# A graph network with routed experts: one row a node sent twice, shares computed beside the slots, a matrix loaded ahead of the last fronts

## The chip, the core and the metric

The kernel runs on one core of a Trainium2 chip. The metric is the device time of one execution in microseconds, the median over runs; less is better.

## What is computed

The reference adds eight layers to `x` (3125 nodes, 256 features), each on a normalized `x`. Graph layers and feed-forward layers alternate:

```
x = x + _L0_gnn_ref(_layernorm(x), edge_index, ...)   # attention, 4 heads, with loops
x = x + _L0_ffn_ref(_layernorm(x)[None], ...)[0]      # 8 experts, hidden 256, best 2, shares by softmax
x = x + _L1_gnn_ref(...)                              # two attention layers
x = x + _L1_ffn_ref(...)                              # a recurrence over all nodes
x = x + _L2_gnn_ref(...)                              # three convolutions
x = x + _L2_ffn_ref(...)                              # 8 experts, hidden 1024, own norm each, best 2, shares
x = x + _L3_gnn_ref(...)                              # one convolution
x = x + _L3_ffn_ref(...)                              # 8 experts, hidden 512, best 2, no shares
```

An expert layer picks for each node the two experts with the highest scores and adds their outputs, weighted by the shares where there are shares. Three blocks have experts: the first, the third and the fourth.

## The kernel before

Nodes lie in 25 tiles of 128 rows, the last with 53. `x` stays on the chip. A program fixes the order of the work: instructions run in order on each engine, and the pieces of different steps are laid between each other by hand, as lists of small functions.

**Fronts** (`Experts.front`, L2075). As soon as a graph layer has finished some node tiles, the front of the expert layer takes them: `norm` normalizes the rows into a tile `rows` (L2071), `turn` transposes them for the scores and makes a second copy of the row on ScalarE (L2098), `route` finds the best two experts (L2104 to L2125), `place` counts the nodes in front of each one and gives every choice a row of the table `slots` in device memory (L2127 to L2149), and `send` writes the two copies of a row there, by two indirect transfers of POOL for a tile (L2194). Each copy carries in its last column the row of `results` that its output goes to (L2149). The table has 3328 rows for each expert. `clear` (L2184) zeroes the rows behind each expert's last one. The sends use eight views of the table in turn, and a transfer waits until the one before it in the same view has landed. A front takes four tiles in the first block (`few=4`, one buffer of `rows`) and two in the others (two buffers). A buffer can be written again when its sends have landed.

**Where the fronts run.** In the first block they are pieces in the list `rest` that `sweep` pops between steps of the attention, and in POOL's queue their sends stand among the gathers of edges (L1826). `finish_apart` starts one when four tiles are done, `finish` when a group of four is (L931 to L972). The first tiles of the attention are dense matmuls (L903, L909) on values that VectorE makes (L846); the other tiles are gathered. In the third and fourth blocks `convolve_rows` (L1388) gives each piece a step of its loop at which it is due. What is left at the end of the loop comes after it (L1444). Then `plan` (L2301) computes the schedule of slots (`schedule`, L2206) and the shares (`weights`, L2276).

**Slots** (`Experts.run`, L2306). There are 56 slots of 128 rows. A loop has five steps, each for another slot: `load` reads the rows by SP at a place that `schedule` gave (L2339), `turn` transposes them, `expand`, `grow` and `shrink` are the two matmuls with the Gelu between (L2380, L2397, L2405), and POOL scatters the output to `results` (L2411). Afterwards the results are read back and added with the shares (L2455).

**Weights.** `open_weights(0)` loads the first matrices of all experts during the graph layer, eight transfers by SP (L2050). The fourth block loads the second ones then too. In the first and third block the second matrices don't fit beside the graph layer's tiles, and `run` loads them, ahead of the first slot in SP's queue.

Of the kernel before, what the change touches and what calls it, by code (L numbers as in the profile page):

```python
# [32 lines left out]
P = 128  # L33
# [22 lines left out]
EACH = NP + P  # L56
FOUR = 4
# [24 lines left out]
class Net:  # L82
    def __init__(self, ctx, tc, w, out):
# [19 lines left out]
        self.slots = dram.tile([E * EACH, D + 1], F32, name="slots")  # L103
# [775 lines left out]
    def attend4(self, ctx, name, psum, hv, target, loops, need, flag, done, rows, times,  # L879
# [52 lines left out]
        def finish_apart(t, acc):  # L932
# [3 lines left out]
            first = t - (t - apart.start) % 4  # L936
            if ready and (t == NT - 1 or t - first == 3):
                apart.rest += ready(psum, first, t - first + 1)
# [4 lines left out]
        def finish(t0, n, acc):  # L943
# [26 lines left out]
            if ready:  # L970
                pieces += ready(psum, t0, n)
# [44 lines left out]
    def gnn0(self, experts):  # L1016
        nc, x = self.nc, self.x
        with ExitStack() as ctx:
# [5 lines left out]
            with ExitStack() as inner:  # L1024
# [11 lines left out]
                z = pc.tile([P, D + 1], F32, name="z")  # L1036
# [39 lines left out]
            with ExitStack() as inner:  # L1076
# [5 lines left out]
                experts.plan(self.pool(inner, "g0plan", 1))  # L1082
# [305 lines left out]
    def convolve_rows(self, cpool, accp, loops, hs, done, ready, loads, apart=None):  # L1388
# [55 lines left out]
        for _, piece in loads + waiting:  # L1444
            piece()

    def gcn(self, name, weights, biases, loops, experts, gather=True):
# [3 lines left out]
        with ExitStack() as ctx:  # L1451
            c = self.pool(ctx, name + "const", 1)
            last = self.pool(ctx, name + "hs", 1)
            cpool = self.pool(ctx, name + "c", 3)
            accp = self.pool(ctx, name + "acc", 2, space=PSUM)
            psum = self.pool(ctx, name + "ps", 3, space=PSUM)
            places = Gathered.pools(self, ctx, name) if gather else None
            shape, kind = ([P, NT, PARTS, D], BF16) if gather else ([P, NT, D], F32)
            experts.begin(ctx)
            inner = ctx.enter_context(ExitStack())  # L1460
# [133 lines left out]
            self.convolve_rows(cpool, accp, loops, hs, add, ready, loads, apart)  # L1594
# [355 lines left out]
class Experts:  # L1950
# [11 lines left out]

    def __init__(self, net, ctx, name, hid, router, w1, b1, w2, b2, bias=None, gain=None,
                 shift=None, keep_tokens=False, weighted=True, store=False,
                 few=2):
# [4 lines left out]
        self.ctx, self.few, self.mats = ctx, few, [None, None]  # L1970
# [22 lines left out]
        self.rows_to = c.tile([P, NT, 2], F32, name="rowsto")  # L1993
        nc.gpsimd.iota(
            self.rows_to, pattern=[[2 * P, NT], [1, 2]], base=0, channel_multiplier=2,
# [5 lines left out]
        self.regs = c.tile([1, SLOTS, 4], I32, name="regs")  # L2001


        if few != 2:
            self.zeros = c.tile([P, FOUR * (D + 1)], F32, name="zeros")
            nc.vector.memset(self.zeros, 0.0)
# [28 lines left out]
    def begin(self, ctx):  # L2035

        self.wk = self.net.pool(ctx, self.name + "front", 2)
        self.big = self.net.pool(ctx, self.name + "frontrows", 4 // self.few)
# [21 lines left out]
    def normalized(self, src, dsts):  # L2060

        nc, n = self.nc, len(src)
        mv = self.wk.tile([P, self.few, 2], F32, name="mv")
# [11 lines left out]
    def front(self, psum, t0, n):  # L2075
# [126 lines left out]
        if self.sent == NT:  # L2202
            pieces.append(clear)
# [97 lines left out]
    def plan(self, pool):  # L2301

        self.schedule(pool)
        self.weights(pool)
# [290 lines left out]
```

## Time and profile before

| | us |
|---|---|
| median of 4 runs | 5177.46 |
| lowest, highest | 5167.13, 5186.29 |
| the profiled execution | 5172.7 |
| its span, first to last instruction | 5170.9 |
| first block: sweep's last matmul, first slot loaded | about 905.5, 969.2 |
| third block: last matmul of the convolution, first matmul of a slot | about 3796.8, 3855.8 |
| fourth block: first slot loaded | 4821.0 |
| slot loops of blocks 1, 3, 4 | about 970 to 1165, 3858 to 4385, 4825 to 5116 |

In a timeline a line is: start, length, engine, source line, operation, output<-input, count, and in brackets how long the engine was idle before and what ended it. In the chain a line is: start, length, what the time went to. "issue" is waiting that the profile can't put down to anything. SPq is SP's queue. Instruction names carry the kernel's tile names: `rows<-x` writes a front's rows, `slots<-rows` sends them, `slots<-slots` loads a slot.

### The profile page before, as it was taken

The page shows a single profiled execution, that of the slowest core. Times are in us where ns is not written, and L with a number is a line of the kernel's source. Part 1 is how long each engine was busy: PE and PEld are TensorE (multiplying, and loading weights), DVE is VectorE, ACT ScalarE, POOL GpSimd, SP SyncE. Part 2 cuts the span into 40 slices and gives each one's busy share as a digit, 9 for nine tenths or more (in the row PEclk, how much of TensorE's full clock was granted, in tenths as well). Part 3 has the DMA queues.
Part 4 walks back from the last instruction along what each step waited for, and adds up shares of the span by engine and source line. Part 5 has one row for each costly group of instructions (what it writes and reads, how often), then busy time and mean ns, then how long its engine had stood idle before and what let it go on. Part 6 is the DMA issues. An engine that isn't in the chain of part 4 may idle for free. (4 is left out here: it accounts for less than half of the span.)

```text
span 5170.9 us, 79417 instructions
## 1 busy us (share of the span) xinstructions
PE 4138.0 (80%) x29365; PEld 2351.5 (45%) x29365; DVE 2431.2 (47%) x7697; ACT 1030.7 (20%) x3048; POOL 1715.7 (33%) x1662
## 2 busy tenths in 40 slices
PE   5867788586998799999998778787649998666795
PEld 3434343453444466744444434344325555433453
DVE  8945555446555455676677311114342222523333
ACT  2411111221011100243333101000013333100231
POOL 2067774223766263000001343534521111344211
PEclk8888888797999899999998988888769999778897
DMA  3243333233333444000000344444431112534213
GB/s 110 81 133 96 97 90 70 89 89 111 109 94 89 97 129 96 2 2 2 2 2 26 110 122 120 127 135 148 108 115 33 30 29 82 156 109 101 57 50 102
DMA packets 351817, 433.30 MB, mean 84 GB/s; under 512 B 74454, under 2 KB 286114, under 8 KB 351427
## 3 DMA queue, kind: packets, MB, share of 16 engines
q0 software_dynamic: 78720, 213.50, 15.2%
q1 hardware_dynamic: 249491, 191.44, 12.7%
q10 hardware_dynamic: 23216, 23.17, 1.4%
q8 instruction: 244, 4.00, 0.3%
q14 instruction: 146, 1.20, 0.1%
HBM read 341.19 MB, written 88.37 MB: 83 GB/s over the span
## 5 line engine op out<-in xcount | busy, mean ns | idle before, releaser
L1826 POOL DMA_INDIRECT edge<-scored,from x780 | 856.5, 1098 | 682.2 <-issue 207.5
L1906 POOL DMA_INDIRECT edge<-rows,from x480 | 460.5, 959 | 477.5 <-PE edgeacc L1941 209.9
L1862 PE MATMUL edgeacc<-edge,weight 128*32 128x65 f32 (+1 forms) x5280 | 424.4, 238 | 145.6 <-issue 110.3
L1862 PEld LDWEIGHTS edgeacc<-edge,weight 128*32 128x32 f32 x5280 | 347.1, 115 | 265.6 <-issue 175.6
L2411 POOL DMA_INDIRECT results<-y,to x168 | 163.7, 974 | 873.5 <-DVE y L2410 680.7
L2405 PE MATMUL py<-w,ht 128*128 x1568 | 429.1, 388 | 13.5 <-DVE y L2410 8.4
L1370 PE MATMUL acc<-c,hs 128*128 128x512 bf16 (+1 forms) x1500 | 374.2, 391 | 60.7 <-issue 59.1
L1648 PE MATMUL pz<-lstm_v,hist 128*32 128x192 f32 x7120 | 384.2, 334 | 26.7 <-DVE hist L1746 7.2
L2380 PE MATMUL ph<-w,xt 128*128 x896 | 387.9, 566 | 20.9 <-ACT xt L2362 14.9
L1415 PE MATMUL acc<-hs,c 128*128 128x512 bf16 x950 | 359.8, 418 | 55.2 <-issue 55.0
L2397 ACT ACTIVATE ht<-pt,par 128x128 f32<-128x128 f32 x784 | 267.5, 367 | 435.2 <-PE pt L2394 425.7
L1419 PE MATMUL acc<-hs,c 128*128 128x256 bf16 x950 | 278.8, 294 | 43.3 <-issue 42.5
L2405 PEld LDWEIGHTS py<-w,ht 128*128 128x128 f32 x1568 | 258.1, 190 | 67.8 <-DVE y L2410 26.9
L2194 POOL DMA_INDIRECT slots<-rows,sloti x150 | 157.5, 1050 | 366.4 <-DVE sloti L2148 188.8
L1681 PE MATMUL pz<-pre,ident 128*128 128x192 f32 x900 | 269.3, 382 | 11.4 <-PEq L1754 11.4
L1648 PEld LDWEIGHTS pz<-lstm_v,hist 128*32 128x32 f32 x7120 | 186.4, 109 | 179.8 <-DVE hist L1746 147.0
L1370 PEld LDWEIGHTS <-hs 128*128 128x128 bf16 x1500 | 150.2, 102 | 254.8 <-issue 124.5
L1773 POOL MEMSET hall<- 128x128 f32 x1 | 0.2, 205 | 788.2 <-DMA L_gnn_b<-in_L_gnn_b 788.2
L2385 DVE COPY h<-ph 128x512 f32<-128x512 f32 (+1 forms) x224 | 139.9, 625 | 216.0 <-PE ph L2380 193.5
L2380 PEld LDWEIGHTS ph<-w,xt 128*128 128x128 f32 x896 | 159.1, 193 | 174.0 <-issue 116.0
L991 PE MATMUL acc<-g1bhv,v 128*128 128x257 f32 x850 | 203.8, 395 | 20.7 <-DVE v L846 13.2
L846 DVE SCALAR_TENSOR_TENSOR v<-q,g1ahv,c 128x512 f32<-128x512 f32 (+1 forms) x300 | 197.0, 702 | 45.2 <-PE acc L909 28.6
(477 smaller groups left out, 6311.2 us busy)
## 6 DMA issues: line engine op xcount, KB each, us to landing
c<-ct SPq DMA_DIRECT2D x106, 640.0 KB
slots<-slots SPq DMA_DIRECT2D x168, 128.5 KB
got<-results SPq DMA_DIRECT2D x24, 768.0 KB
w<-in_L_ffn_W SPq DMA_DIRECT2D x16, 1024.0 KB
ct<-cols SPq DMA_DIRECT2D x6, 2400.0 KB
c<-ct SPq DMA_DIRECT2D x30, 480.0 KB
edge<-scored,from POOLq DMA_INDIRECT x780
rows<-new ACTq DMA_DIRECT2D x20, 512.0 KB
```

What stands on the lines that cost most here:

```text
L991: nc.tensor.matmul(a[:, : D + 1], v[0][:, j * P : (j + 1) * P], hv[:, s, 0, : D + 1], start=(s == 0), stop=(s == NT - 1),)
L1370: made = self.nc.tensor.matmul(acc[f][:, : n * P], lhs, cols[s], start=(s == 0 and i == 0), stop=(s == NT - 1), skip_group_check=True,)
L1415: nc.tensor.matmul(acc[t], lhs, hs[:, s, 0:2, :].rearrange("p i d -> p (i d)"), start=start, stop=stop, skip_group_check=True,)
L1419: return nc.tensor.matmul(acc[t][:, D:], lhs, hs[:, s, 2, :], start=False, stop=stop, skip_group_check=True,)
L1648: made = nc.tensor.matmul(pz[q * R : (q + 1) * R, :], s, m, start=start, stop=stop, tile_position=(0, q * R),)
L1681: made = nc.tensor.matmul(pz, self.ident, pre[:, g, s, :], start=True, stop=False)
L1826: nc.gpsimd.indirect_dma_start(out=tile[:, j, :], out_offset=None, in_=self.rows, in_offset=bass.IndirectOffsetOnAxis(ap=index, axis=0),)
L1862: nc.tensor.matmul(state["acc"][g * GROUP : (g + 1) * GROUP, at : at + width + 1], m[:, j, h, :], rows[:, j, h, : width + 1], start=(j == ...
L1906: self.net.nc.gpsimd.indirect_dma_start(out=tile, out_offset=None, in_=self.rows, in_offset=bass.IndirectOffsetOnAxis(ap=index, axis=0),)
L2380: nc.tensor.matmul(ph[:, :wide], st["xt"][:, k, :], st["w1"][:, k * hid + c0 : k * hid + c0 + wide], start=(k == 0), stop=(k == KD - 1),)
L2397: nc.scalar.activation(ht[:, m, :], pt[:, cut], AF.Gelu, bias=st["par"][:, m : m + 1])
L2405: nc.tensor.matmul(py[:, :D], st["ht"][:, m, :], st["w2"][:, m * D : (m + 1) * D], start=(m == 0), stop=(m == nhc - 1),)
```

## The change

A row is kept once, with two more columns instead of one: the result row of the first choice, and the table row of the second. Both sends of a node send the same row. In the slot loop a new VectorE instruction compares the second column with the slot's own table rows (`self.numbers`, computed in `schedule`) and adds 1 to the result row where they are equal. `rows` has three buffers everywhere, in a pool of its own. All fronts take two tiles (`PAIR`). `clear` comes after the last sends, with a tile of zeros of its own. `weights` moves into the slot loop, at its sixth turn (`i == 5`). In the first block the second matrix is loaded after the second slot. In the third block the convolution's tiles are released as soon as its last matmuls are in the program, and the second matrix is loaded there, ahead of the pieces of fronts that are left.

```diff
-            first = t - (t - apart.start) % 4
-            if ready and (t == NT - 1 or t - first == 3):
+            first = t - (t - apart.start) % PAIR
+            if ready and (t == NT - 1 or t - first == PAIR - 1):
                 apart.rest += ready(psum, first, t - first + 1)
...
-            if ready:
-                pieces += ready(psum, t0, n)
+            for j in range(0, n if ready else 0, PAIR):
+                pieces += ready(psum, t0 + j, min(PAIR, n - j))
...
-                experts.plan(self.pool(inner, "g0plan", 1))
+                experts.schedule(self.pool(inner, "g0plan", 1))
...
-        for _, piece in loads + waiting:
-            piece()
+        return [piece for _, piece in loads + waiting]
...
-            self.convolve_rows(cpool, accp, loops, hs, add, ready, loads, apart)
+            rest = self.convolve_rows(cpool, accp, loops, hs, add, ready, loads, apart)
+            held.close()
+            if loops:
+                rest = experts.open_weights(1) + rest
+            for piece in rest:
+                piece()
...
-        self.big = self.net.pool(ctx, self.name + "frontrows", 4 // self.few)
+        self.big = self.net.pool(ctx, self.name + "frontbig", 2)
+        self.sends = self.net.pool(ctx, self.name + "frontrows", 3)
...
-            rows = got["rows"] = self.big.tile([P, few, 2, D + 1], F32, name="rows")
-            to = [rows[:, j, 0, :D] for j in range(n)]
+            rows = got["rows"] = self.sends.tile([P, few, D + 2], F32, name="rows")
+            to = [rows[:, j, :D] for j in range(n)]
+            nc.vector.tensor_copy(rows[:, :n, D : D + 1], self.rows_to[:, ts, :])
...
-            nc.scalar.copy(got["rows"][:, j, 1, :D], got["rows"][:, j, 0, :D])
...
-            nc.vector.tensor_copy(got["rows"][:, :n, :, D], self.rows_to[:, ts, :])
+            nc.vector.tensor_copy(got["rows"][:, :n, D + 1 :], slots[:, :, 1:])
...
-                    in_=got["rows"][:m, j, r, :], in_offset=None,
+                    in_=got["rows"][:m, j, :], in_offset=None,
...
-        if self.sent == NT:
-            pieces.append(clear)
-        return pieces + [lambda j=j: send(j) for j in range(n)]
+        pieces += [lambda j=j: send(j) for j in range(n)]
+        return pieces + [clear] if self.sent == NT else pieces
...
+        nc.vector.tensor_scalar(self.numbers, start, self.place, None, op0=ALU.add)
...
-            if self.mats[1] is None:
-                for load in self.open_weights(1):
-                    load()
+            second = self.open_weights(1) if self.mats[1] is None else []
             if not planned:
-                self.plan(net.pool(ctx, self.name + "plan", 1))
+                self.schedule(net.pool(ctx, self.name + "plan", 1))
+            pool = net.pool(ctx, self.name + "weights", 1)
...
+                own = wk.tile([P, 1], F32, name="own")
+                nc.vector.scalar_tensor_tensor(
+                    own, st["rows"][:, D + 1 :], self.numbers[:, i : i + 1],
+                    st["rows"][:, D : D + 1], op0=ALU.is_equal, op1=ALU.add,
+                )
-                nc.vector.copy_predicated(mine, self.valid[:, i : i + 1], st["rows"][:, D : D + 1])
+                nc.vector.copy_predicated(mine, self.valid[:, i : i + 1], own)
...
+                if i == 1:
+                    for piece in second:
+                        piece()
+                if i == 5:
+                    self.weights(pool)
```

The pools of the convolution are opened in a stack `held` of their own so that it can be closed early. Not shown: the widths of the table and its rows (D + 2 columns), the tile of zeros, and the general path, which does not run here.

## The prediction

> **What bounds the kernel now.** I read the page first, for the span and the chain that ended last, then that chain in order of time around the places where fronts end and slots begin, then the timeline there, then the waits and busy times of the stretches between.
>
> ```profile
> span 5170.9 us, 79417 instructions
> PE 4138.0 (80%) x29365; PEld 2351.5 (45%) x29365; DVE 2431.2 (47%) x7697; ACT 1030.7 (20%) x3048; POOL 1715.7 (33%) x1662
> PE 17%; issue 14%; another core or an unknown queue 6%; DVE 5%; DMA 3%; POOL 2%; ACT 1%; SPq 0%; ACTq 0%; DVEq 0%; POOLq 0%
> ```
>
> PE is the busy engine, and the change leaves its large matmuls alone. So the change can earn only where PE stands idle: at the three places where a block's last fronts must be placed, sent and landed before its first slot can be read. The chain, from block 3's last fronts (start, length, what):
>
> ```profile
> 3803.91 6.15 DMA slots<-rows,sloti
> ...
> 3813.29 2.91 DMA slots<-rows,sloti
> ...
> 3824.30 4.06 DMA slots<-rows,zeroto
> 3828.55 0.37 SPq L2050
> ...
> 3834.14 2.90 SPq L2050
> ...
> 3847.13 8.59 DMA slots<-slots
> ```
>
> To be seen: sends, then clearing, then eight loads of the second matrix, 1024 KB each and some 2.9 us apart, and only behind them, in the same queue, the first slots. The same place in block 4, whose matrices are there already, and then PE's first slot of block 3, from the timeline:
>
> ```profile
> 4816.50 0.97 POOL L2184 DMA_INDIRECT slots<-rows,zeroto  x1 [0.30 <-issue]
> 4820.96 0.36 SPq L2339 DMA_DIRECT2D slots<-slots  x1
> 4823.29 0.66 PE L2351 MATMUL tp<-ident,slots 128*128 128x128 f32 x2 [14.25 <-DMA slots<-slots]
> ```
> ```profile
> 3855.76 0.47 PE L2351 MATMUL tp<-ident,slots 128*128 128x128 f32 x1 [39.90 <-DMA slots<-slots]
> ```
>
> From the landing of the last clear to PE's first slot: 4823.29 - 4820.96 = 2.3 us in block 4, 3855.76 - 3828.55 = 27.2 us in block 3. The rest of block 3's is the matrix. Block 1's end:
>
> ```profile
> 909.68 0.17 DVE L2149 COPY rows<-rowsto 128x2 f32<-128x2 f32 x1 [10.03 <-DMA slots<-rows,sloti]
> 926.75 0.17 DVE L2149 COPY rows<-rowsto 128x8 f32<-128x8 f32 x1 [5.15 <-DMA slots<-rows,sloti]
> 963.55 0.97 POOL L2194 DMA_INDIRECT slots<-rows,sloti  x1 [0.30 <-issue]
> 969.16 0.37 SPq L2339 DMA_DIRECT2D slots<-slots  x1
> ```
>
> VectorE stands still, twice, until earlier sends have left the one buffer of rows, and everything behind L2149 in its queue stands with it.
>
> **The change, part by part** (minus is time won).
>
> A. *Block 3's second matrix moves ahead of the last fronts.* Its memory is that of the tables and features, whose last matmul (L1415 on hs) ends near 3796.8. SP's queue is empty then (its last table load was issued at 3781.8), so nothing is passed but the slots. 8.39 MB at 348 GB/s (the DMA view's rate from 3834 to 3855) is 24.1 us. Ten sends (132 KB each) and the clears, 2.4 MB, share the engines: 6.8 us more, so the matrix has landed at 3796.8 + 24.1 + 6.8 = 3827.7. The sends: the last clear goes out at 3824.30; two VectorE stalls before it (6.16 at 3813.15, 0.50 at 3816.57) go with part D, so 3817.6. A landing takes 4.25 us here and 4.46 in block 4, but 5.6 in block 1 (963.55 to 969.16), where 2 MB of matrix ran beside it; I take 5.6, 3823.2. The later of the two, 3827.7, plus 2.3 us is 3830.0 against 3855.76: **-25**. Bounds: -30 if the slots don't queue behind the matrix (3823.2 + 2.3); -10 if the full queue doubles each landing and the sends wait for their views of the table (16 us given back).
>
> B. *Block 1's end.* With three buffers L2149 no longer waits. Of the 10.03 us only 5.9 are won: the node tile's transposes then come at the end of the sweep's matmuls, 905.5 instead of 911.4. The second stall, 5.15, is whole: 11.05 together. Two pairs instead of one group of four let the first sends go earlier; POOL has eleven indirect transfers to issue at 1.28 us, 14 us, whatever comes first. I take 3 us for that: -14 (between -5, the second stall alone, and -19). Against it, the second matrix now stands behind two slot loads in SP's queue. Before, its eight issues (4.49 us at 957.95) lay under the wait for the sends. Now they push the third slot's load from 3.4 us after the first (972.56) to 7.9, and 2.1 MB at 348 GB/s, 6.0 us, go ahead of it: landed some 11.7 us after the first load, where its transposes began after 8.4. The first matmul on the matrix came 10.1 us after that load (979.22) and would wait until about 11.2. +2.5 (0 to +8). Together **-11.5**.
>
> C. *Block 4's end.* L2071 waited 8.72 us until 4801.95 for a buffer. Without it the last sends follow the eight earlier ones (POOL until 4803.1, 0.3 us between) instead of starting at 4810.47: **-7** (-9 to -4, by how long POOL's own waits for landings then last).
>
> D. *The other stalls of this kind*: 6.98 at 757.9, 3.18 at 3612.4, and 0.46, 7.27, 15.39, 3.31 in block 4 before 4708: 36.6 us. The chain holds 4.52, 3.96, 4.70 and 3.88 us of sends there, 17.1; during the 15.39 it runs through PE. What is late next is PE's own queue. **-8** (-17 to 0).
>
> E. *Shares inside the slot loop.* Moved, not removed: seven VectorE instructions (0.36, 0.36, 0.42, 0.35, 0.17, 0.30, 0.35) and six of 0.35 in blocks 1 and 3, 4.5 us each, six in block 4, 2.1: 11 us. At the plan they stood beside POOL's sends (block 1's plan was done at 957.9, its sends at 969.2), so leaving wins nothing. In the loop VectorE has room, but the Exp stands between Gelus: two more table loads in blocks 1 and 3 each, at 1.28 us (the row at 975.56 below), 5.1 us of ScalarE. PE waits for ScalarE's xt each slot. **+5.5** (0 to +17: all of it laid end to end).
>
> ```profile
> 975.56 1.28 ACT L2397 ACT_TABLE_LOAD   x1
> 970.00:1165.00 195.00, 166.09 (x747) 112.90 (x747) 80.78 (x287) 58.67 (x169) 54.45 (x56) 0.95 0.30 88
> 3858.00:4385.00 527.00, 512.12 (x1977) 300.84 (x1976) 137.35 (x326) 189.41 (x559) 54.78 (x56) 0.99 0.13 39
> ```
>
> (Columns of the last two: stretch, us, busy us of PE, weight loads, VectorE, ScalarE, POOL, clock, DMA.) The Trainium skill speaks against this part: "ScalarE: Activation LUTs", section "Table sets: the hidden batching unit", says to do all calls of one function set before switching, and "What ACT_TABLE_LOAD costs" there gives some 2.66 us a switch, the load and a drain. By that page the four switches would be 10.6 us instead of 5.1, and the sum 5.5 us worse if none is hidden; the trace shows the 1.28 only.
>
> F. *One more VectorE instruction a slot* (who owns the row), 168 times; not in this trace. Its neighbours on one column: 0.152 (L2366) and 0.214 (L2365), so 26 to 36 us of VectorE, which is busy 81 of 195, 137 of 527 and 96 of 291 us in the three loops. Cover: PE. Without cover +36. **+3** (0 to +36), nearest to the loops' VectorE, free over half the time.
>
> G. *Block 1's fronts in pairs*: 13 instead of 7. A front of four costs 5.6 us of VectorE beside what goes by node (12 instructions for the root at 0.16, 2.45 for routing, 1.2 for placing), a pair about 5.0: 13 x 5.0 - 7 x 5.6 = 26 us more. Each front also waits for PE twice. From the waits of VectorE in the sweep (total, times, longest):
>
> ```profile
> DVE pos L2135 <- PE tp L2133: 18.1, 5, 5.8
> DVE logits L2112 <- PE tp L251: 15.8, 3, 6.7
> DVE logits L2112 <- remote: 5.7, 1, 5.7
> ```
>
> That is 39.6 us over six fronts, so six more add up to +40 if PE starves meanwhile. PE is the one that is late in these waits, and it waited for VectorE's v for only 14.5 us from 440 to 900: **+5** (-5, if shorter bursts serve the sweep better, to +40).
>
> H. *Hidden*: 75 ScalarE copies go (0.41 each; ScalarE is 1% of the chain), 45 more small VectorE copies come (33 before, 13 x 3 x 2 after, 0.17 each; VectorE waits at the ends), a row grows from 1028 to 1032 bytes. POOL's number of transfers stays, the clears now stand behind the last sends, and the row is written once. 0 (-3 to +7).
>
> Sum: -25 - 11.5 - 7 - 8 + 5.5 + 3 + 5 = **-38**. The profiled execution took 5172.7 us (span 5170.9): 5135. It lies 4.8 us under the median of the runs, 5177.46, inside their spread of 19.
>
> **The rivals.**
>
> *More is won* (chance 0.16). A, B, C and D at their good ends, G at nothing: -30 - 16.5 - 9 - 17 + 5.5 + 3 = -64, 5109. For it: the stalls stand in the chain. Against: a stall's end usually meets the next wait.
>
> *The matrix is paid elsewhere, the change doesn't do what it says* (0.14). The load fills the DMA engines under the last sends; the landings get longer, POOL waits for views, the first slots wait as before: A at -10, D at 0, B at -6: -10 - 6 - 7 + 13.5 = -9.5, 5163. For it: POOL already waits for landings at 3810 and 3813. Against: block 1's landing beside a load grew by only 1.3 us.
>
> *Slower: POOL held by sends that wait* (0.10). POOL's queue is in order, and gathers of edges stand behind sends. Before its sends POOL waited for the slot numbers (L2148) 12 times, 188.8 us in all, 15.7 each. Block 1 gets six more places where a send can arrive too early. While gathers are the limit (440 to 640: 128 transfers, 145.7 us busy and 0.3 us between, 184 of 200) such a wait is lost whole: six are +94, the total -38 - 5 + 94 = +51 with G's 5 left out, 5224. It decides from 2.7 such waits (43 over 15.7). Against: five gathered tiles are ahead of their use, and in the sweep only one such wait (45.1 us) fell from 640 to 900.
>
> **How the numbers follow.** The forecast, 5135, has 0.60; its own range is 5112 to 5165. Within 0.3% of the median is 5162 to 5193, about what a measurement of this kernel can tell from no change. Faster: 0.58 of the forecast's 0.60 and the first rival's 0.16, 0.74. Same: the rest of the forecast and the second rival, 0.16. Slower: 0.10. The range is 5100 to 5180: the first rival's time with A to D a little better still, the hidden case with F's or E's costs on top; outside lie the slower case and some of the extremes.
>
> **What would show it.** A: the loads of the matrix (L2050's) start near 3797 on the old scale and PE's first slot comes 4 to 12 us after the last clear went out, not 31. B, C, D: no VectorE wait on sends ahead of the rows; first slot of block 1 some 14 us earlier after the sweep's last matmul. E: two table loads more in each weighted loop, one longer slot. F: loops of 195, 527 and 291 us grow by under 2 us each. G: the sweep from 440 to 900 keeps its length to 10 us. The prediction is wrong if a loop grows by 10 us, if POOL idles before sends in the sweep, or if the first slot still waits behind the matrix.

## The result, and the profile after

The kernel after took 5182.55 us (median of 44 runs, 5164.77 to 5203.23) against 5178.17 (70 runs, 5157.22 to 5196.34): ratio 1.001, interval 1.0003 to 1.0018. A gain was forecast; what came is no change to speak of. The forecast, 5135, is missed by 48 us, and the time lies 2.5 us above the range.

The page of after, first lines: span, then busy time, share and instructions of each engine.

```profile
span 5177.9 us, 79194 instructions
PE 4151.5 (80%) x29389; PEld 2366.4 (46%) x29389; DVE 2470.7 (48%) x8063; ACT 1005.6 (19%) x2973; POOL 1696.9 (33%) x1662
```

The span is 7.0 us longer. TensorE's busy time is 13.5 us longer than before (4138.0) and its idle time 6.5 us shorter, so the page doesn't tell where the 7 us come from. The stretches do, cut at the same events, in us:

| stretch | before | after | difference |
|---|---|---|---|
| start to the sweep's last dense matmul | 905.5 | 907.8 | +2.3 |
| to block 1's first slot transposed | 66.0 | 61.8 | -4.2 |
| to its first matmul on the second matrix | 7.8 | 10.9 | +3.1 |
| block 1's loop, from there to the last | 172.6 | 177.2 | +4.6 |
| results, block 2 | 1650.3 | 1653.2 | +2.9 |
| block 3: convolutions, to their last matmul | 994.7 | 1002.1 | +7.4 |
| to its first slot | 59.0 | 34.7 | -24.3 |
| to its first matmul on the second matrix | 17.3 | 17.2 | -0.1 |
| block 3's loop | 505.3 | 522.8 | +17.5 |
| results | 45.7 | 47.8 | +2.1 |
| block 4: convolution | 364.8 | 364.0 | -0.8 |
| to its first slot | 34.4 | 30.1 | -4.3 |
| its loop, results | 347.6 | 348.4 | +0.8 |

Part A came to the forecast number. From the timeline of after, SP's loads of the second matrix, the first slot, and TensorE's first work on it:

```profile
3812.88 20.88 SPq L2055 DMA_DIRECT2D w<-in_L_ffn_W  x8
3845.30 0.36 SPq L2336 DMA_DIRECT2D slots<-slots  x1
3847.58 0.45 PE L2348 MATMUL tp<-ident,slots 128*128 128x128 f32 x1 [20.47 <-DMA slots<-slots]
```

The eight loads start with the end of the last convolution (3812.9), and 11 us lie between them and the first slot, which now waits for the clears. The chain of after there:

```profile
3821.10 8.47 DMA slots<-rows,sloti
...
3829.83 6.34 DMA slots<-rows,sloti
...
3838.80 6.49 DMA slots<-zeros,zeroto
3845.30 2.15 DMA slots<-slots
```

Sends and clears end last, and beside the matrix they take longer to land than in before (in the chain of before 6.15 and 2.91 us for the sends, 4.06 for the clear).

Blocks 1 and 4 show what B and C became. Timeline of after, the ends of the fronts there:

```profile
954.99 0.97 POOL L2187 DMA_INDIRECT slots<-zeros,zeroto  x1 [0.30 <-issue]
958.48 0.17 DVE L2212 TENSOR_TENSOR count<-upto,first 128x8 f32<-128x8 f32 x1 [7.30 <-DMA slots<-zeros,zeroto]
965.67 0.23 DVE L2277 TENSOR_SCALAR numbers<-start,place 128x56 f32<-128x56 f32 x1
967.30 0.38 SPq L2336 DMA_DIRECT2D slots<-slots  x1
...
4819.70 0.20 POOL L2224 IOTA number<- 128x56 f32 x1
4819.93 0.62 DVE L2234 TENSOR_TENSOR past<-number,last 128x448 f32<-128x448 f32 x1 [5.04 <-issue]
4827.26 0.36 SPq L2336 DMA_DIRECT2D slots<-slots  x1
```

The last clear goes out 8.6 us earlier than the last send of before (963.5). But the plan begins only when the clears have read their zeros: its tiles lie in the memory that the zeros' pool gave back. Then the plan's 7.4 us, which had lain beside the sends, stand in the open. In block 4 the plan's number rows stand behind the clears in GpSimd's queue.

The loop of block 3 is the great loss. TensorE's timeline there, first of before, then of after, the start of one slot:

```profile
4098.11 0.27 PE L2351 MATMUL tp<-ident,slots 128*128 128x128 f32 x1
4098.22 0.38 PE L2394 MATMUL pt<-ident,h 128*128 128x128 f32 x2
4098.43 0.27 PE L2419 MATMUL tp<-ident,sel 128*8 128x128 f32 x1
4098.79 0.70 PE L2405 MATMUL py<-w,ht 128*128 x2
4099.32 0.27 PE L2351 MATMUL tp<-ident,slots 128*128 128x128 f32 x1
```
```profile
4114.25 0.27 PE L2348 MATMUL tp<-ident,slots 128*128 128x128 f32 x1
4114.36 0.38 PE L2396 MATMUL pt<-ident,h 128*128 128x128 f32 x2
4114.58 0.27 PE L2421 MATMUL tp<-ident,sel 128*8 128x128 f32 x1
4115.12 0.33 PE L2348 MATMUL tp<-ident,slots 128*128 128x128 f32 x1 [0.27 <-ACT xt L2353]
```

In every second slot the pair of py matmuls (py is the product with the second matrix) that lay between a slot's two transpositions is gone, and the second transposition waits for ScalarE's copy of the first. TensorE's waits in the whole loop (waited for: total, times, longest):

```profile
PE tp L2348 <- ACT xt L2353: 10.5, 29, 0.5
```

In before it was 0.3, once. TensorE is idle for 22.4 us of this loop in after, for 7.7 in before. Nobody wrote that order. The text ahead says that the program fixes the order of the work; that holds for the order in which it hands over its pieces, while the build lays out each engine's instructions from it. How the build chooses is not shown by any run.

### The profile page after: what moved, and what is told of

Read it like the earlier page. It is cut to its first block, busy times and chain, and to the rows that moved or that the text cites. A ratio compares the mean times of both kernels' runs of the same rounds, so it can differ in the third digit from the quotient of the medians.

```text
span 5177.9 us, 79194 instructions
## 1 busy us (share of the span) xinstructions
PE 4151.5 (80%) x29389; PEld 2366.4 (46%) x29389; DVE 2470.7 (48%) x8063; ACT 1005.6 (19%) x2973; POOL 1696.9 (33%) x1662
## 3 DMA queue, kind: packets, MB, share of 16 engines
q1 hardware_dynamic: 249491, 191.53, 12.6%
## 5 line engine op out<-in xcount | busy, mean ns | idle before, releaser
L1832 POOL DMA_INDIRECT edge<-scored,from x780 | 838.9, 1075 | 699.6 <-issue 207.9
L2407 PE MATMUL py<-w,ht 128*128 x1568 | 424.1, 387 | 16.5 <-DVE y L2412 13.7
L2382 PE MATMUL ph<-w,xt 128*128 x896 | 387.5, 565 | 26.3 <-ACT xt L2359 15.7
```

The costliest lines, as they stand in the source:

```text
L1832: nc.gpsimd.indirect_dma_start(out=tile[:, j, :], out_offset=None, in_=self.rows, in_offset=bass.IndirectOffsetOnAxis(ap=index, axis=0),)
L2382: nc.tensor.matmul(ph[:, :wide], st["xt"][:, k, :], st["w1"][:, k * hid + c0 : k * hid + c0 + wide], start=(k == 0), stop=(k == KD - 1),)
L2407: nc.tensor.matmul(py[:, :D], st["ht"][:, m, :], st["w2"][:, m * D : (m + 1) * D], start=(m == 0), stop=(m == nhc - 1),)
```

## The experiments

A ratio stands against the kernel before on the same chip. That kernel took 5214 us on the chip of the first set, 4720 to 4724 on those of the next three, 5176 on that of the last.

**First set: what lengthened the loop, and what block 1's end waits for.** Pools alone (`held` and its `close()`, but `experts.open_weights(1)` stays in `run`):

```diff
+            held = ctx.enter_context(ExitStack())
+            last = self.pool(held, name + "hs", 1)
...
+            held.close()
             for piece in rest:
```

> The kernel before, with one part of the change alone: the pools of the tables and features stand in a stack of their own that closes ahead of the last fronts, and the second matrix still comes behind the fronts. Theory (order): block 3's slot loop grew by 17.6 us because this regrouping changes the order of the instructions on TensorE in the loop (the second transposition of a slot's rows now comes before a matmul of the slot three earlier, and waits for ScalarE's copy of the first). Then this kernel, without any new instruction in the loop, has a loop of 520 to 525 us from its first to its last matmul where the kernel before has 505.3 (first py to last py), and the time is 15 to 20 us above before. Rival (VectorE): the loop grew because of the added VectorE instruction; then the loop stays at 504 to 507 and the time within 5 us of before.

Ratio 1.0008 (0.9993 to 1.0024). The loop took 522.2 us with no new instruction in it, and TensorE waits as in after:

```profile
PE tp L2354 <- ACT xt L2359: 10.3, 28, 0.5
```

The time missed the expectation because the free memory alone lets the matrix go earlier: 39.7 us from the last convolution to the first slot instead of 59.0, so one gain and one loss of nearly the same size.

The early load as well (`rest = experts.open_weights(1) + rest`):

> The kernel before with part A alone: pools regrouped and block 3's second matrix ahead of its last fronts. Both theories: the stretch from the last matmul of the third convolution to PE's first slot falls from 59.1 us to 33 to 39. Theory (order): the loop of block 3 grows by 15 to 20 us as in the kernel after, so the time is only 3 to 10 us under before. Rival (VectorE): the loop stays at 505 and the time falls by 20 to 26 us.

Stretch 40.1 and loop 522.3, as the order theory has it. The total missed: ratio 1.0014 (0.9996 to 1.0032), some 8 us above before instead of 3 to 10 under. The profile puts 12 us into the sweep, where the program is that of before (624.0 to 636.5 in three profiles of it on this chip), and 3 into the convolutions. But the profiled execution (5234.4) was itself 12 us above the median of its runs (5222.6), so the long sweep is its own, and the 8 us of the median aren't accounted for.

One more instruction a slot, in the kernel before:

```diff
+                own = wk.tile([P, 1], F32, name="own")
+                nc.vector.scalar_tensor_tensor(
+                    own, st["rows"][:, D : D + 1], 0.0, st["rows"][:, D : D + 1],
+                    op0=ALU.mult, op1=ALU.add,
+                )
```

> The kernel before with one more VectorE instruction a slot in front of the predicated copy (the row number times 0 plus itself), in the place where the change puts the one that tells whose the row is; 168 in all. The instructions on TensorE keep the order of before. Theory (order): it lies beside TensorE's work; the loops of 171.3, 505.3 and 280.0 us (first to last py) grow by under 2 us each and the time by 0 to 4 us. Rival (VectorE): block 3's loop grows by 12 us or more and the time by 15 to 30.

Loops 173.6, 505.3, 279.2; ratio 1.0000 (0.9985 to 1.0015). The instruction costs nothing that shows; the order costs the 17 us. The rival is out.

Zeros in memory of their own:

```diff
+        if self.hid != 1024:
+            self.zeros = self.net.pool(ctx, self.name + "clear", 1).tile(
```

> The kernel after, with the zeros of the clears in memory of their own in blocks 1 and 4, taken when the fronts begin, instead of memory that the plan then takes over. Theory (memory): in block 1 the plan waited 7.30 us for the clears to have read the zeros, and behind it the first slot's load came 12.3 us after the last clear was issued; with memory of its own the plan's number rows lie at the start and the load comes 4 to 6 us after the clear, so block 1's first slot comes 6 to 9 us earlier against the sweep's end and the time falls by 5 to 9 us against after. In block 4 the number rows still stand behind the clears in GpSimd's queue, so nothing moves there. Rival (landing): the first slot waits for the sends to land whatever the plan does; the first slot stays 14 to 15 us behind the last clear and the time stays within 2 us of after.

First slot 54.5 us after the sweep instead of 61.8, 6.1 behind the last clear; ratio 0.9987 (0.9972 to 1.0002). The waits of B were as worked out for the first slot; the plan's new wait had eaten the gain. At the end of block 1's loop nothing of it is left: 246.2 us from the sweep's end to the last py, 246.3 in before.

**Second set: mending.** Both transpositions first:

```diff
                 for k in range(KD):
                     nc.tensor.transpose(pt[:, k * P : (k + 1) * P], ...)
-                    if self.own: nc.scalar.activation(xt[:, k, :], ...)
+                for k in range(KD if self.own else 0):
+                    nc.scalar.activation(xt[:, k, :], ...)
```

> The kernel after, with both transpositions of a slot's rows emitted ahead of ScalarE's two copies, so that the second transposition no longer stands behind the first copy (blocks 3 only has two copies; the others are unchanged). Theory (order): TensorE's waits for ScalarE's xt ahead of the second transposition, 10.5 us in 29 waits in the loop of after against 0.3 in before, go, and block 3's loop (first to last py) falls from some 522 us to 505 to 514; the time falls by 8 to 17 us against after. Rival (bandwidth): the loop is longer because the slots' loads, results and 4 KB of other traffic are served later, whatever TensorE's order; then the loop stays above 518 us.

Loop 504.6; ratio 0.9977 (0.9968 to 0.9986). TensorE still waits 10.3 us for ScalarE, now ahead of ph, so the wait alone isn't the 18 us: the two transpositions also take 0.44 us together where they took 0.27 and 0.33 apart.

Block 1's matrix first again:

```diff
             second = self.open_weights(1) if self.mats[1] is None else []
+            for piece in second:
+                piece()
+            second = []
```

> The kernel after, with block 1's second matrix issued ahead of its first slot again. Theory: in after the matrix behind two slot loads costs twice: PE's first matmul on it comes 10.9 us after the first transposition instead of 7.7, and the loop from first to last py is 177.1 us instead of 172.6, because its start gives the instructions on TensorE another order. Here both go back, 7.5 to 8.5 and 170 to 174.5 us, and the time falls by 5 to 8 us against after; the first slot itself doesn't come later, since the eight issues lie under the plan. Rival (VectorE): the loop is longer by the added instruction and stays at 176 to 178.

First py 7.2 us after the first slot and a loop of 172.4, as expected, but the first slot came 69.1 us after the sweep: the eight issues wait for the plan's memory and stand in the open. Up to the last py it is 248.7 us against 251.1 in the run before, a gain of 2.4 where 5 to 8 were expected. Ratio 1.0027 (1.0017 to 1.0038), which holds block 3's longer loop.

Fours in block 1 again:

```diff
-            first = t - (t - apart.start) % PAIR
+            first = t - (t - apart.start) % 4
...
-        few = PAIR
+        few = self.few
```

> The kernel after, with block 1's fronts in groups of four nodes again, still with three buffers of rows. Theory: the pairs cost some VectorE time in the sweep (250.2 us busy from 440 to 900 in before, 259.0 in after) that TensorE and the gathers cover, so the sweep (first to last dense matmul, 624.6 in before, 625.1 in after) stays within 6 us, VectorE's busy time there falls back to 247 to 253 us, and the time stays within 5 us of after. Rival (pairs): each of six more fronts is paid by some 4 us of TensorE's idle time; then the sweep is 15 to 30 us shorter than that of the other kernels of this set.

Ratio 1.0043 (1.0031 to 1.0056). The sweep took 556.5 us, with pairs 536.0 and 536.8: pairs win 20 us here, so the theory (within 6 us) missed and the rival had the wrong sign.

Four mends: zeros apart, both transpositions first, block 1's matrix first, and the plan of blocks 3 and 4 in memory at the other end.

```diff
+                with tc.using_default_side("right"):
+                    plan = net.pool(ctx, self.name + "plan", 1)
```

> The kernel after with four edits: zeros of the clears in memory of their own in blocks 1 and 4, the plan of blocks 3 and 4 in memory at the other end (so that it waits for no clear), both transpositions ahead of ScalarE's copies, and block 1's second matrix ahead of its slots. Theory: the sum of the four against after: -7 (block 1's end, as measured), -4 (block 4's first slot 5 us behind its last clear instead of 10.8), -8 to -17 (block 3's loop), -5 to -8 (block 1's start and loop) = -24 to -36, some 20 to 30 us under before, ratio to before 0.994 to 0.996. Rival: a stall taken away meets the next one; then less than half of it, ratio 0.998 or more.

Ratio 0.9975 (0.9965 to 0.9985), short of it. Block 1 to the last py 239.8, block 3's loop 504.8 and block 4's start 25.7 came in, but block 4's first weights (`L_gnn_W`) were loaded only as block 3's results ended, not some 500 us ahead as in the other runs of this set, the first matmul on them came 12.6 us after the results instead of 22 ahead of their end, and the convolution ended 333.1 us after block 3 instead of 313 to 315. The plan's memory is the only edit that this run has alone; the mended kernel of the next set, without it, has 316.5.

**Third set: one layout against the other.** After itself; after with zeros apart, both transpositions first, and the number rows among the constants; before with the early matrix and both transpositions first; before with pairs. The new edits:

```diff
+        number = self.number = c.tile([P, SLOTS], F32, name="number")
+        nc.gpsimd.iota(
...
-        "L0_ffn_b2", keep_tokens=True, few=4,
+        "L0_ffn_b2", keep_tokens=True,
```

> The kernel after itself, on the chip of the three that follow, as their yardstick: its stretches outside the gathering stages as in its own profile within 2 us (block 1's first slot 61.8 us after the sweep's last dense matmul, block 3's first slot 34.7 us after the last matmul of the convolutions, block 3's loop 522.8, block 4's first slot 30.1 after its convolution), and a ratio to before of 1.000 to 1.003.

> The kernel after with three edits, without the one that delayed block 4's convolution: the clears' zeros in memory of their own in blocks 1 and 4, the plan's number rows built once with the constants (so that GpSimd's queue doesn't hold them behind the clears), and both transpositions ahead of ScalarE's copies. Theory: block 1's first slot comes 53 to 56 us after the sweep instead of 61.8, block 3's loop takes 503 to 507 us instead of 522.8, block 4's first slot comes 24 to 27 us after its convolution instead of 30.1, nothing else moves by more than the gathering stages scatter: 27 to 32 us less than after, ratio to before 0.994 to 0.997. Rival: as with the four edits of the run before, something else in the order or the memory moves and gives back more than 10 us of it; then the ratio is above 0.997.

> The kernel before with part A alone (pools regrouped, block 3's second matrix ahead of the last fronts) and both transpositions ahead of ScalarE's copies. Theory (order): part A keeps its gain of some 19 us at block 3's start and no longer loses 17 in the loop: loop 503 to 507, ratio to before 0.995 to 0.998. Rival: part A costs 5 us or more elsewhere, in the three convolutions (they were 3 to 6 us longer in the kernels with regrouped pools than in the one without on the same chip); then the ratio is 0.998 or more though the loop is short.

> The kernel before with one part of the change alone: block 1's fronts in pairs instead of fours, with two copies of each row and two buffers. Theory: pairs help or cost nothing in the sweep (on a chip where the gathers were fast the fours made it 20 us longer); where the gathers limit it the sweep stays within 8 us of the others here, and the ratio to before is 0.996 to 1.001. Rival (pairs): 13 fronts cost TensorE's idle time; the sweep is 12 us or more longer than that of the early-matrix kernel of this set, which has fours, and the ratio is above 1.002.

Ratios: after 1.0021 (1.0012 to 1.0030), after mended 0.9958 (0.9944 to 0.9971), early matrix 0.9974 (0.9963 to 0.9985), pairs alone 0.9932 (0.9919 to 0.9946). The mended one has the three stretches expected (54.6, 504.4 and 25.5 us). Pairs, thought to cost 5 us, are the best single part: sweep 535.1 against 555.8 with fours, first slot 58.1 behind it against 66.5. And something in after still lost: the stages of the convolutions of blocks 3 and 4 took 785.3 and 314.7 us there, 772.5 and 300.7 in the early-matrix kernel, 766.9 and 295.6 with pairs. Waits of after in block 4's stage on this chip, of TensorE and of VectorE:

```profile
PE tp L235 <- DVE rows L2076: 58.2, 6, 17.0
DVE rows L2091 <- DMA slots<-rows,sloti: 103.8, 10, 21.6
```

In the kernel with pairs they are 27.2 and 83.7: three buffers had not ended the stalls, they had more. One of them, from the timeline of after in its first profile:

```profile
4638.94 0.83 DVE L2076 TENSOR_SCALAR rows<-x,mv,rstd 128x256 f32<-128x256 f32 x2
4646.22 0.95 POOL L1912 DMA_INDIRECT edge<-rows,from  x1 [0.30 <-issue]
4647.48 1.00 POOL L2197 DMA_INDIRECT slots<-rows,sloti  x1 [0.31 <-issue]
...
4652.84 0.17 DVE L2091 COPY rows<-rowsto 128x2 f32<-128x2 f32 x1 [13.08 <-DMA slots<-rows,sloti]
4661.51 0.17 DVE L2115 TENSOR_TENSOR logits<-tp,L_ffn_bg 128x16 f32<-128x16 f32 x1 [8.49 <-PE tp L252]
```

In the program as built, the copy L2091 that stands between a front's normalization and its scores belongs to the front two later. It needs no data, only a buffer, and the build puts it as far ahead as there are buffers: three such copies stand in VectorE's queue, from 4451 to 4461, ahead of the stage's first normalization at 4483. Its buffer is that of the front before the one in work, whose last three sends (from 4647.48) stand behind twenty gathers in GpSimd's queue. So a third buffer only moves the copy one front further ahead.

**Fourth set: pin the copy**, alone and with the mends, in after and in before.

```diff
-            nc.vector.tensor_copy(rows[:, :n, D : D + 1], self.rows_to[:, ts, :])
...
             nc.vector.tensor_copy(got["rows"][:, :n, D + 1 :], slots[:, :, 1:])
+            nc.vector.scalar_tensor_tensor(
+                got["rows"][:, :n, D : D + 1], slots[:, :, 1:], 0.0, self.rows_to[:, ts, :],
+                op0=ALU.mult, op1=ALU.add,
+            )
```

> The kernel after, in which the copy of the row's number into the rows takes one of the slot numbers as an operand too (times 0, plus the row number), so that it can't be carried out before the front's slots are known. Theory (queue): VectorE's stalls on sends in the convolutions of blocks 3 and 4 (some 89 and 104 us in after on the chip of the last set, 24.5 and 42.6 on that of its own profile, all at this copy) come because the copy, ready as soon as a buffer is free, stands in VectorE's queue ahead of the front in work, and waits for sends that stand behind some twenty gathers in GpSimd's queue. Pinned, it waits for nothing, and with three buffers the normalisation that now writes the rows first finds a free one: the stalls fall under a third, TensorE's waits for the rows there likewise, and the time is 20 to 45 us less than after where the gathers are fast (before some 4720 us), 3 to 15 us where they are slow (before some 5200). Rival (buffers): the wait is for a buffer, whoever asks first; then it moves to the normalisation with the same length, and the time stays within 5 us of after.

> The kernel after with the pinned copy, the clears' zeros in memory of their own in blocks 1 and 4, the plan's number rows built once with the constants, both transpositions ahead of ScalarE's copies, and block 1's second matrix ahead of its slots. Theory: what the single edits gave adds up: against after -7 to -11 for block 1 from the sweep's end to the last py, -18 for block 3's loop, -4.6 for block 4's start, and whatever the pinned copy gives; ratio to before 0.985 to 0.993 where the gathers are fast, 0.992 to 0.997 where they are slow. Rival: the stall moves on; ratio 0.994 or more where they are fast.

> The kernel before with the copy of the row's number pinned behind the slot numbers in the same way, and nothing else; two buffers of pairs (one of four nodes in block 1). Theory (queue): VectorE's stalls at this copy go here too, and what is left is the wait of the normalisation for one of only two buffers; TensorE's waits for the rows in the convolutions of blocks 3 and 4 fall by at least half, the time by 10 to 30 us where the gathers are fast, 2 to 10 where they are slow. Rival (buffers): no change within 5 us; then it takes the third buffer as well as the pin.

> The kernel before with four edits: block 1's fronts in pairs, block 3's second matrix early, both transpositions ahead of ScalarE's copies, and the pinned copy; still two copies of a row and two buffers. Theory: pairs alone gave -30 where the gathers are fast, the early matrix with the short loop -10, the pin what it gives in the kernel before with the pin alone: ratio 0.985 to 0.992 there, 0.993 to 0.998 where they are slow. Against the kernel after with all mends it tells what one copy and a third buffer are worth.

Ratios: pinned 0.9774 (0.9760 to 0.9787), with all mends 0.9705 (0.9691 to 0.9719), before pinned 0.9845 (0.9830 to 0.9859), before mended 0.9770 (0.9755 to 0.9784). The queue theory holds, with more than twice the gain expected: no stall at this copy is left, and none at the normalization, in the convolutions of after pinned. TensorE's wait in block 4's stage:

```profile
PE tp L235 <- DVE rows L2076: 0.9, 2, 0.6
```

In before pinned the wait moves to the normalization in part (26.3 and 40.7 us in the two stages, their last fronts included), still worth 74 us. What two buffers and two copies of a row cost where the gathers are fast is read from four profiles of this set: the two stages together take 998.8 and 997.3 us in the two kernels of before, 976.4 and 975.6 in the two of after. In after without the pin, in the set before, they took 1100.0. So the copy's place was the larger part of it, in both kernels, and the buffers and copies the smaller.

**Last set: two buffers, and the first kind of chip.** In the second kernel no edit is new.

```diff
-        self.sends = self.net.pool(ctx, self.name + "frontrows", 3)
+        self.sends = self.net.pool(ctx, self.name + "frontrows", 2)
```

> The kernel after with the pinned copy and two buffers of rows instead of three (one copy of a row each, as in after). Theory (both needed): with the pin and two buffers of two copies the kernel before kept 26 and 41 us of stalls in the convolutions of blocks 3 and 4, at the normalisation; with three buffers and the pin nothing was left. Here 20 to 50 us a stage come back at the normalisation, these two stages are together 15 to 25 us longer than with three buffers where the gathers are fast, and the ratio to before is 0.980 to 0.984 there (0.992 to 0.998 where TensorE's granted clock in the convolutions is near 0.84, as on the chip of the first profiles). Rival (pin alone): the third buffer does nothing once the copy is pinned; no stalls, ratio 0.976 to 0.979 where the gathers are fast.

> The kernel after with the pinned copy, the clears' zeros in memory of their own in blocks 1 and 4, the plan's number rows built once with the constants and both transpositions ahead of ScalarE's copies; block 1's second matrix stays behind two slot loads, as in after. Theory: block 1 from the sweep's last dense matmul to the last py takes 245 to 251 us, where the same kernel with the matrix ahead took 240.0; everything else as there, so the time is 5 to 11 us above it: ratio 0.971 to 0.974 where the gathers are fast, 0.989 to 0.996 where TensorE's clock in the convolutions is near 0.84 (there TensorE itself is late and the stalls that the pin takes away were short). Rival: the place of the matrix makes no difference here, 240 to 243 us.

This chip was slow in the convolutions, so whether the third buffer is needed where the gathers are fast was not answered. Two buffers and the pin: ratio 0.9973 (0.9954 to 0.9992), with a stall left only ahead of each stage's last sends (6.59 and 7.32 us), first slots 36.9 and 35.7 us after the convolutions instead of 35.2 and 30.2 in the pinned kernel with three. All mends with the matrix behind: 0.9894 (0.9864 to 0.9923), block 1 to its last py 244.5 us against 240.0 with the matrix ahead. On both kinds of chip the mended kernel beats before and after.

## Why the prediction failed, by its steps

Forecast were -38 us, the two profiles differ by +7.0. Of these 45 us the slot loops of blocks 1 and 3, which were to grow by under 2 us each, make some 19 beyond F's own +3, D 15, B and C 13; E and G were 10 too dear; some 8 lie in A and in stretches without a term.

- **A, -25**: -24.3. The move works as told, but what ends last is another thing, and the closeness of the number is partly luck. The prediction let the matrix land last, 30.9 us after the convolution, and the sends and clears 26.4 after it. In the chain of after the clears end last, 32.4 us after it: GpSimd waited for landings (2.55 and 1.34 us), the last clear went out 25.9 us after the convolution instead of 20.8, and landings beside the matrix took 6.3 to 8.5 us, reckoned at 5.6.
- **B, -11.5, and C, -7**: -1.1 (-4.2 and +3.1) and -4.3. The stalls did go. Not seen, a term put at nothing, was the wait that took their place: the plan in the zeros' memory, 7.30 us in block 1, and its number rows behind the clears in block 4. With both mended, block 1's first slot comes 11 us earlier than in before (55.0) and block 4's 8.8 (25.6): up to the first slot the sizes worked out were sound. The matrix behind two slots cost 3.1 ahead of the first py, forecast 2.5, and more in the loop (F): in that mended kernel block 1 up to its last py takes 244.5 us, only 1.8 less than before.
- **D, -8**: +6.6 over both stages (+7.4 and -0.8). The step that failed is "With three buffers L2149 no longer waits", which D takes over for "The other stalls of this kind": the prediction read the stalls at L2149 as a want of buffers, said that everything behind L2149 stands with it, and didn't ask which front the waiting copy belonged to. VectorE's stalls on sends in the two stages rose from 29.6 us in before to 67.1 in after. How much of the +7.4 is theirs is not separated; the regrouped pools, below, may be a part. With the copy pinned and even two buffers the two stages take 991.8 and 348.7 us on the last chip, 19 us less than in before (one profile each).
- **E, +5.5**: nothing. The program calls `weights` in the loop, but the build puts its instructions where their data are ready: shares are computed from 943.16 to 951.17, as before beside the sends. The table loads in the three loops are two, as before; so the rule on batching functions that the prediction weighed was never put to the test.
- **F, +3**: the sentence that failed most is "loops of 195, 527 and 291 us grow by under 2 us each". The instruction itself costs some 1 us at most (loops of 173.6, 505.3 and 279.2 with it, 172.6, 505.3 and 280.0 without). But block 3's loop grew by 17.5 and block 1's by 4.6, and the cause is another part: the memory freed early in block 3, the late matrix in block 1. With each the build laid out another order of TensorE's instructions, and the prediction, which counted only what was added, had no term for that. Its own sign, a loop that grows by 10 us, is what came.
- **G, +5**: +0.6 here, within scatter, and -20 where the convolutions run fast. The waits that the 40 us were worked out from did grow (39.6 us before, 73.4 after, from 440 to 900), but TensorE didn't starve meanwhile: its wait for VectorE's v there fell from 14.5 us to 0.3. What goes with the 20 us on the fast chips is GpSimd's wait for a front's slot numbers in the sweep: one of 33 to 35 us in the three profiles with fours, one of 10 to 16 us in the nine with pairs. It was not changed alone, so this is not shown. VectorE's stalls on sends are not the cause: fours with three buffers had none in the sweep and took 556.5.
- **H, 0**: held. What is left of the table, +6 in all, lies in block 2, in the results and in block 4's loop.

Of the rivals none came as told. The slower one, sends that hold GpSimd, had the right queue and half of the circle. In the sweep its waits stayed (45.1 us before, 43.4 after). In the convolutions the gathers hold the sends, the sends hold VectorE's copy, and the front behind the copy then comes late with the next slot numbers: GpSimd's waits for them in the two stages, 34.4 and 28.9 us in after on a fast chip, were 2.6 and none with the copy pinned.

Three things stay open: what the third buffer is worth alone where the gathers are fast; whether regrouping the pools costs some 5 us in block 3's convolutions on the slow chips (1022.7 to 1025.8 us with it, 1017.5 without, one profile each; on a fast chip 726.4 with and 731.2 without); and why an early memory gives the build another steady order.

## What to carry to other kernels

Where a build orders the instructions, the order is part of the change: compare each engine's instructions in the loops before and after, not only what was added. An instruction that needs only a buffer is put far ahead, and its wait then holds everything behind it; give it an operand that ties it to its place before adding buffers. Scratch memory that is given back is taken by what comes next, and that then waits for the last transfer that reads it.

## What was not expected of the hardware

The same program differs by 9% between chips, and all of it lies in the graph stages (the recurrence of block 2 takes 658.9 and 658.5 us). Each set of runs had a chip of its own; that it is the chip, and not the hour, was not tested apart. Block 3's convolution stage (stretch, us, busy us of PE, weight loads, VectorE, ScalarE, POOL, clock, DMA share, GB/s) of after in its first profile and of after on a fast chip:

```profile
2810.80:3812.90 1002.10, 744.99 (x4129) 396.31 (x4125) 285.08 (x1063) 83.95 (x190) 399.32 (x416) 0.84 0.41 119
```
```profile
2639.50:3424.80 785.30, 666.33 (x4056) 381.31 (x4125) 287.41 (x1063) 83.87 (x189) 398.05 (x416) 0.93 0.51 152
```

On the first kind TensorE is granted 0.84 of its clock, and its waits of the kind "issue", for nothing that the profile shows, add up to 145 us; on the other chip it is 0.93 and 2 us. VectorE's and GpSimd's busy times are equal within 1%. Block 3's loop takes the same on both (522.8 and 522.4). VectorE's stalls on sends are shorter on the first, too (24.5 and 42.6 us in the stages of blocks 3 and 4 of after, 88.9 and 103.8 on the other). So such a stall is cheap on the one chip, where TensorE is late anyway, and dear on the other: the pinned copy with the other mends gives 1.1% on the first kind and some 3% on the second (there with block 1's matrix ahead of its slots).

With the stalls gone TensorE's granted clock rose, too: in block 4's stage 0.85 in after, 0.94 in after pinned (last lines: after on its fast chip, after pinned on its own):

```profile
4047.00:4361.70 314.70, 230.20 (x1452) 143.67 (x1480) 130.42 (x592) 21.52 (x56) 158.05 (x170) 0.85 0.42 119
```
```profile
3977.10:4233.70 256.60, 233.30 (x1452) 140.74 (x1480) 131.07 (x588) 21.49 (x56) 157.95 (x170) 0.94 0.53 146
```

The Trainium skill, "TensorE: Matmul & The Clock Gate", section "HAM oscillation — how this bites in real kernels", says that idle gaps of more than some 3.4 us let the clock fall again. The first of these two stages shows it gap by gap. TensorE stood idle there five times for 9.7 to 17.0 us, and each time the granted clock was 0.50 for 13.7 to 17.1 us, from 2 to 5 us after the work had stopped until 3 to 6 us after it went on. The last of them, the end of the gap and the stretch at 0.50:

```profile
4329.18 0.66 PE L235 MATMUL tp<-ident,rows 128*128 128x128 f32 x2 [16.99 <-DVE rows L2076]
4315.10:4332.10 17.00, 2.92 (x10) 1.60 (x11) 1.13 (x5) 0.37 (x1) 8.66 (x9) 0.50 0.51 81
```

In after pinned the longest idle time of the stage, behind its first 2 us, is 1.9 us. The clock still falls to 0.50 three times there, for 3.4 to 10.2 us, and for these the traces give no reason.
